# A graph network on one core: the TensorE share of the row fetch is dealt over another chunk's work, with more columns, and reaches the edge network

## The chip, the cores and the metric

One core of a Trainium2 chip runs the kernel. The metric is the device time of one execution in microseconds (us). A core has TensorE (PE, with its weight loads shown apart as PEld), VectorE (DVE), ScalarE (ACT), GpSimd (POOL) and SyncE (SP); each works through its own instructions in order, and semaphores join them. The profile shows one execution.

## The reference

The graph has 12,500 nodes with 32 features and 400,000 edges, sorted by their destination. Three attention layers run one after the other, then a LayerNorm with the residual, then an edge network with a maximum over each node's edges, then a second LayerNorm.

```python
def _gat(x, edge_index, W, att_s, att_d, bias, heads, ch, neg_slope):
    h = (x @ W.T).reshape(n, heads, ch)
    a_s = (h * att_s[None]).sum(-1)
    a_d = (h * att_d[None]).sum(-1)
    logits = leaky_relu(a_s[src] + a_d[dst], neg_slope)
    m = segment_max(logits, dst)
    ex = exp(logits - m[dst])
    denom = segment_sum(ex, dst)
    alpha = ex / (denom[dst] + 1e-16)
    out = segment_sum(alpha[:, :, None] * h[src], dst)
    return out.reshape(n, heads * ch) + bias
...
h = _gat(x, ..., heads=2, ch=16)      # then scale, elu, clip
h = _gat(h, ..., heads=2, ch=16)      # then elu, clip
x = layernorm(x + _gat(h, ..., heads=1, ch=32))
e_feat = concatenate([x[src], x[dst], edge_attr])
v = relu(e_feat @ W1 + b1) @ W2 + b2
x = layernorm(x + maximum(segment_max(v, dst), x))
```

## The kernel before

**Tiling.** Edge `p*3125 + t` lies in partition `p`, column `t`. A *column* is thus 128 edges, one in each partition, and there are 3125 of them. Every stage works through the columns in 54 *chunks*: 50 of 60 columns, then 48, 32, 29 and 16. Since the edges are sorted by destination, segment sums and maxima are scans along a partition, carried from chunk to chunk; layer 2 and the edge network walk backwards, so that the runs of one layer end where those of the next begin.

**The fetch.** For each column a layer needs the row of each edge's source: h and the scores, 36, 34 or 33 numbers in layers 1 to 3, and 32 numbers in the edge network (buffer `xs`). There are two ways to get it.

- `gather` (L71): one indirect DMA on POOL per column, 128 rows from a table in memory.
- `Fetch` (L221 to L275), for one column in `EVERY`: all 98 x 128 node rows are held in SBUF as `by_group`, three bf16 parts in 7 groups. A matmul with the identity lays the sources out as a row (L255, fp32, two passes); DVE compares them into one-hot weights `oh` (L258); 21 bf16 matmuls, 7 groups by 3 parts, add up into the PSUM tile `acc` (L270); DVE masks out the right one of 14 rows, `mine` (L273), and reduces it into the column's place in the buffer (L275). With its weight loads a column is 46 PE instructions.

`by_group` is filled from x ahead of layer 1 and by `node_groups` (98 gathers and the splitting into parts) ahead of layers 2 and 3.

**A layer** is `attention`. The function `rows_of(c + 1)` issues the gathers of the next chunk into one of three buffers `g`, and then calls `fetch`, which writes all PE columns of that chunk in one block, ahead of the present chunk's own operations. Then chunk c is worked on: scores, running maximum, exponentials, the weighted rows `gf` (L833, one for each head, the last reader of `g`), their scans (L839), the sums' rows copied out (L842 and what follows it), and `finish`: division, bias, ELU, and for blocks of 16 columns the product with the next layer's weights (`ph`, L620) and attention vectors (`pa`, L621). Layer 3 ends in `finish3` and `layernorm` in place of the products. A buffer `g` may be filled again when its L833 is through.

**The edge network**, `edge_network`, fetches every column on POOL, into one of four buffers `xs`. For each chunk DVE spreads the destination's rows over its edges with scans (`xf`, L958 and L968), then, for each block of 16 columns, turns three inputs (`xt` L974, `et` L975, `xst` L976), PE multiplies them (`ph`, L981, twelve passes and as many weight loads with the two halves of the hidden layer), ACT applies the relu (`ht`, L983), PE makes `pv` (L987), DVE turns it back (L988). After the blocks come the maximum scans (L991), the result (L906 to L908) and the LayerNorm (L633 to L641).

**Order.** The engines' orders come from a scheduler that works on the program's order, so that part of a block of columns is found between the present chunk's operations. Within an engine the order is then fixed, and an instruction that waits holds up those behind it.

Of the kernel before, what the change touches and what calls it, by code (L numbers as in the profile page):

```python
# [24 lines left out]
def gnn_resnorm_kernel(ctx: ExitStack, tc: tile.TileContext, a: dict, out: bass.AP):  # L25
# [24 lines left out]
    T = 60  # L50
# [39 lines left out]
    EVERY = {1: 7, 2: 7, 3: 7}  # L90
# [18 lines left out]
    runs = ctx.enter_context(tc.tile_pool(name="runs", bufs=1))  # L109
    gstack = ctx.enter_context(ExitStack())  # L110
    xpool = gstack.enter_context(tc.tile_pool(name="x", bufs=1, side="right"))
    by_group = xpool.tile([P, 3, KT, KN * (D + 4)], BF16, name="by_group")
# [36 lines left out]
    zeros = const.tile([P, 500], F32, name="zeros")  # L149
# [70 lines left out]

    class Fetch:  # L221
# [22 lines left out]
        def fetch(self, psum, g, t0, n, bufs=2):  # L244

            todo = [t for t in range(t0, t0 + n) if t in self]
            if not todo:
                return
            pool, w, i0 = self.pool, self.w, todo[0] // self.every
            bm = pool.tile([P, 9, KN], F32, name="bm")[:, :len(todo), :]  # L250
            nc.vector.tensor_tensor(bm, bcast(count[:, None, :KN], [P, len(todo), KN]),
                                    bcast(self.b[:, i0:i0 + len(todo), None], [P, len(todo), KN]), op=ALU.is_equal)

            def ones_of(m):
                nc.tensor.matmul(places_p, lhsT=bcast(self.at[:, i0 + m:i0 + m + 1], [P, P]), rhs=ident,  # L255
                                 start=True, stop=True)
                oh = pool.tile([P, KT, P], BF16, name="oh")
                nc.vector.tensor_tensor(oh, bcast(places_p[:, None, :], [P, KT, P]),  # L258
                                        bcast(kid[:, :, None], [P, KT, P]), op=ALU.is_equal)
                return oh  # L260

            coming = ones_of(0)
            for m, t in enumerate(todo):
                oh = coming
                if m + 1 < len(todo):
                    coming = ones_of(m + 1)
                acc = psum.tile([P, 512], F32, name="acc", bufs=bufs)[:, :KN * w]
                for k in range(KT):
                    for i in range(3):
                        nc.tensor.matmul(acc, lhsT=oh[:, k, :], rhs=by_group[:, i, k, :KN * w],  # L270
                                         start=(k == i == 0), stop=(k == KT - 1 and i == 2))
                mine = pool.tile([P, D + 4, KN], F32, name="mine")[:, :w, :]
                nc.vector.tensor_mul(mine, acc.rearrange("p (w b) -> p w b", b=KN),  # L273
                                     bcast(bm[:, m:m + 1, :], [P, w, KN]))
                nc.vector.tensor_reduce(g[:, t - t0, :w], mine, axis=AX.X, op=ALU.add)  # L275
# [22 lines left out]
    def clear(table, part=0, parts=1):  # L298
        flat = edge_rows(table).rearrange("p t w -> p (t w)")
        k = TE * table.shape[1] // parts  # L300
        z = next(z for z in range(500, 0, -1) if k % z == 0)
        tc.keep_in_program_order(
            nc.sync.dma_start(out=flat[:, part * k:part * k + k].rearrange("p (k z) -> p k z", z=z),
                              in_=bcast(zeros[:, None, :z], [P, k // z, z])))
# [290 lines left out]
    def finish(li, pool, psum, den, v, n):  # L595
# [8 lines left out]
        nc.scalar.activation(e, e, AF.Exp, scale=-1.0)  # L604
        heads = HEADS[li + 1]
# [3 lines left out]
        for b in range(0, n, TB):  # L609
            nt = min(TB, n - b)  # L610
            w = nt * D
            pe = psum.tile([P, TB * D], F32, name="pe")[:, :w].rearrange("p (f t) -> p f t", t=nt)
            nc.scalar.activation(pe, e[:, :, b:b + nt], AF.Identity, bias=minus[:, 1:2])
            yb = pool.tile([P, TB * D], F32, name="yb", bufs=1)[:, :w].rearrange("p (f t) -> p f t", t=nt)
            nc.vector.scalar_tensor_tensor(yb, y[:, :, b:b + nt], 3.0, pe, op0=ALU.min, op1=ALU.add)
            yt = pool.tile([P, TB * D], F32, name="yt")[:, :w]
            nc.vector.transpose(blocks(yt), yb.rearrange("p f t -> p t f"))  # L617
            ph = psum.tile([P, TB * D], F32, name="ph")[:, :w]
            pa = psum.tile([P, TB * D], F32, name="pa")[:, :w]
            nc.tensor.matmul(ph, lhsT=w_bd, rhs=yt, start=True, stop=True)  # L620
            nc.tensor.matmul(pa, lhsT=a_bd, rhs=yt, start=True, stop=True)  # L621
            at = pool.tile([P, TB, D], F32, name="at", bufs=1)[:, :nt, :]
            nc.vector.transpose(tb[:, b:b + nt, :D], blocks(ph))  # L623
            nc.vector.transpose(at, blocks(pa))  # L624
            nc.scalar.copy(tb[:, b:b + nt, D:], at[:, :, :heads])  # L625
            nc.scalar.copy(ta[:, b:b + nt, :], at[:, :, heads:2 * heads])
        return tb, ta

    def layernorm(lp, st, x, n, sq=None):
# [4 lines left out]
        nc.vector.tensor_scalar(st, st, 1.0 / D, None, op0=ALU.mult)  # L634
        nc.vector.tensor_sub(x, x, bcast(st[:, :, None], [P, n, D]))
        nc.scalar.activation(sq, x, AF.Square)
        nc.vector.tensor_reduce(st, sq, axis=AX.X, op=ALU.add)
        nc.vector.tensor_scalar(st, st, 1.0 / D, EPS, op0=ALU.mult, op1=ALU.add)
        nc.scalar.activation(st, st, AF.Sqrt)
        nc.vector.reciprocal(st, st)  # L640
        nc.vector.tensor_mul(x, x, bcast(st[:, :, None], [P, n, D]))  # L641

    def finish3(pool, psum, den, v, x, n):

        y = psum.tile([P, D * 64], F32, name="y3")[:, :D * n].rearrange("p (f t) -> p f t", t=n)
        divided(3, y, den, v, n)
        nc.vector.tensor_add(x, x, y.rearrange("p f t -> p t f"))
        layernorm(pool, den[:, T:], x, n)
# [73 lines left out]
    def attention(li, idx):  # L722
# [10 lines left out]
        with ExitStack() as stack:  # L733
# [23 lines left out]
            with tc.tile_pool(name=f"ps{li}", bufs=1, space=PSUM) as psp, \  # L757
                    tc.tile_pool(name=f"fps{li}", bufs=1, space=PSUM) as fps:
                den = small_p[:, 128:]
                def rows_of(c):  # L760
# [5 lines left out]
                    fetch.fetch(psp, g, t0, n)  # L766
                    return g
# [3 lines left out]
                for c, (t0, n) in enumerate(todo):  # L771
                    g = coming
                    if c + 1 < len(todo):
                        coming = rows_of(c + 1)
                    (ad, xr) = loaded
# [28 lines left out]
                    nc.vector.scalar_tensor_tensor(lg, lg, slope, lg, op0=ALU.mult, op1=ALU.max)  # L804
                    if c == 0:
# [14 lines left out]
                    nc.scalar.activation(wt, lg, AF.Exp)  # L820

# [6 lines left out]
                    for h in range(heads):  # L828
# [6 lines left out]
                        nc.scalar.copy(v[:, h * wd + ch, cur], wt[:, h, :])  # L835
                        for f in range(0, wd, FS):
# [3 lines left out]
                                                         turned(gf[:, o:o + k], rev), 0.0, op0=ALU.mult, op1=ALU.add)  # L840
                    rows = sp.tile([P, T, gw + heads], F32, name="rows", bufs=1)[:, :n, :]
# [5 lines left out]
                    if li < 3:  # L847
                        tb, ta = finish(li, fp, fps, den, v[:, :, cur], n)
                        nc.sync.dma_start(out=edge_rows(gives[li + 1])[:, t0:t0 + n, :], in_=ta)
                    else:  # L850
                        finish3(fp, fps, den, v[:, :, cur], xr, n)
# [58 lines left out]
    def edge_network(tag, in_order):  # L910


        with tc.tile_pool(name=f"in{tag}", bufs=2) as ip, tc.tile_pool(name=f"gx{tag}", bufs=4) as gp, \
                tc.tile_pool(name=f"v{tag}", bufs=2) as vp, tc.tile_pool(name=f"t{tag}", bufs=2) as tp, \
                tc.tile_pool(name=f"pf{tag}", bufs=1, space=PSUM) as pfp, \
                tc.tile_pool(name=f"ph{tag}", bufs=1, space=PSUM) as php:
# [15 lines left out]

            old = None
            loaded = load(0)
            for c, (t0, n) in enumerate(todo):
                xs = gp.tile([P, T, D], F32, name="xs")
                for t in range(n):
                    gather(xs[:, t, :], tables[4], src_last[:, t0 + t:t0 + t + 1])
# [9 lines left out]
                rf = pfp.tile([P, FS * (T + 1)], F32, name="rf")[:, :FS * m]  # L948
                cft = cf.rearrange("p (k t) -> p k t", t=m)
                rft = rf.rearrange("p (k t) -> p k t", t=m)  # L950
# [4 lines left out]
                nc.vector.memset(rft[:, :, n:], -BIG)  # L955
                nc.scalar.copy(cft[:, :, :n], ct)
                nc.vector.tensor_scalar(rft[:, :, :n], ct, -1.0, BIG, op0=ALU.add, op1=ALU.mult)
                nc.vector.tensor_mul(xft[:, :, :n].rearrange("p f t -> p t f"), xd, bcast(keep[:, :, None], [P, n, D]))  # L958
                if old is None:
# [6 lines left out]
                for f in range(0, D, FS):  # L966
                    fs = slice(f * m, (f + FS) * m)
                    nc.vector.tensor_tensor_scan(turned(xf[:, fs], True), turned(cf, True), turned(xf[:, fs], True), 0.0,  # L968
                                                 op0=ALU.mult, op1=ALU.add)
                for b in range(0, n, TB):  # L970
# [7 lines left out]
                    for h in range(2):  # L978
# [5 lines left out]
                        hts.append(ht)  # L984
                    pv = php.tile([P, TB * D], F32, name="pv")[:, :w]
                    for h in range(2):
                        nc.tensor.matmul(pv, lhsT=w2_bd[:, h, :], rhs=hts[h], start=(h == 0), stop=(h == 1))  # L987
                    nc.vector.transpose(vft[:, :, b:b + nt].rearrange("p f t -> p t f"), blocks(pv))  # L988
                for f in range(0, D, FS):
                    fs = slice(f * m, (f + FS) * m)  # L990
                    nc.vector.tensor_tensor_scan(turned(vf[:, fs], True), turned(rf, True), turned(vf[:, fs], True), 0.0,  # L991
                                                 op0=ALU.add, op1=ALU.max)
                nc.scalar.copy(xd, vft[:, :, :n].rearrange("p f t -> p t f"))
# [9 lines left out]
                layernorm(tp, small_p[:, 128:], z, n)  # L1003
# [58 lines left out]
```

## Time and profile before

| what | us |
|---|---|
| median of 10 executions | 22450.19 |
| lowest and highest | 22433.18 and 22474.39 |
| the profiled execution | 22439.96 |
| its span | 22438.2 |
| setup, up to the first chunk of layer 1 | 0 to 316 |
| layer 1 | 316 to 6150 |
| layer 2 | 6300 to 12126 |
| layer 3 | 12255 to 17535 |
| edge network | 17535 to 22300 |
| merge of the partition ends, rows out to the nodes | 22300 to 22438 |

The stretches between the layers are the filling of `by_group`. In the lists of the profile, a group of instructions shows the line, the engine, the operation, out<-in by the program's names, partitions x elements, and the count; then busy us, the mean ns of one, and after the second bar the idle time of the engine just before these instructions with what ended most of it. In a timeline a row has start and length in us, and in brackets the idle time before it and what ended it. "remote" and "issue" mean that nothing which the profile shows released the instruction. The ends of matmuls are modelled. The granted clock is TensorE's, as a share of full speed.

Two rows on the fetch, beside those that come below:

```profile
L270 PE MATMUL acc<-by_group,oh 128*128 128x504 bf16 (+2 forms) x28098 | 6637.7, 393 | 683.0 <-issue 673.2
L258 DVE TENSOR_TENSOR oh<-fixed,kid 128x896 bf16<-128x896 f32 x1338 | 1446.1, 1081 | 222.8 <-remote 96.9
```

### The profile page before, as it was taken

The numbers are of one execution on the slowest core, as the hardware profiler recorded it, in microseconds if no ns is written. First come the engines' busy times: TensorE is split into PE (matmuls) and PEld (weight loads), VectorE is DVE, ScalarE is ACT, GpSimd is POOL, SyncE is SP. The second block draws the span as 40 slices with busy tenths as digits, with TensorE's granted clock in tenths as the row PEclk, the third lists the DMA queues.
The fourth block names the chain that finished last, engine by engine and source line by source line (L and its number), as shares of the span: only waits on it lengthen the run. The fifth ranks groups of instructions, "written<-read, shape, count | busy, mean of one in ns | idle before, by whom it ended". The sixth has DMA issues, their size and how long they took to land.

```text
span 22438.2 us, 107898 instructions
## 1 busy us (share of the span) xinstructions
PE 9727.2 (43%) x35914; PEld 4508.6 (20%) x35914; DVE 9821.6 (44%) x13987; ACT 2921.2 (13%) x3898; POOL 11186.0 (50%) x11780
## 2 busy tenths in 40 slices
PE   1545555454534444444443344444444233333332
PEld 0222222222212222222221122222222111111111
DVE  2444444444524444444443344444444345555554
ACT  0111111111101111111111010101101111111111
POOL 6444444444354444444445544545444666666663
PEclk5777777777767777777776676676767666666666
DMA  3111111111101111111111111111111111111111
GB/s 50 45 38 38 49 38 38 39 40 29 34 17 28 28 28 30 28 28 30 28 28 31 31 40 37 42 36 42 38 39 41 45 48 59 55 59 55 59 55 43
DMA packets 562459, 881.63 MB, mean 39 GB/s; under 512 B 267999, under 2 KB 482494, under 8 KB 548446
## 3 DMA queue, kind: packets, MB, share of 16 engines
q1 hardware_dynamic: 185036, 665.01, 8.2%
q0 software_dynamic: 376544, 206.39, 6.3%
q8 instruction: 285, 4.67, 0.1%
q10 hardware_dynamic: 304, 3.20, 0.0%
q14 instruction: 290, 2.37, 0.0%
HBM read 370.51 MB, written 503.27 MB: 39 GB/s over the span
## 4 chain that ended last, share of the span: by engine, by line
another core or an unknown queue 34%; DVE 24%; PE 24%; issue 10%; ACT 4%; POOL 3%; DMA 1%; DVEq 0%; SPq 0%; POOLq 0%; ACTq 0%
PE acc L270 15%; PE ph L981 3%; DVE gf L833 3%; DVE gf L839 3%; PE pv L987 1%; DVE oh L258 1%; DVE yt L617 1%; PE ph L620 1%; DVE y L589 1%; DVE mine L273 1%; PE pa L621 1%; PE fixed L255 1%; DVE y L593 1%; DVE z L908 1%
## 5 line engine op out<-in xcount | busy, mean ns | idle before, releaser
L270 PE MATMUL acc<-by_group,oh 128*128 128x504 bf16 (+2 forms) x28098 | 6637.7, 393 | 683.0 <-issue 673.2
L71 POOL DMA_INDIRECT g<-table,src_i x2679 | 2532.5, 945 | 3195.9 <-DVE gf L833 2369.4
L71 POOL DMA_INDIRECT g<-table,src_last x2679 | 2541.8, 949 | 3153.0 <-DVE gf L833 2351.5
L71 POOL DMA_INDIRECT g<-table,src_first x2679 | 2538.3, 947 | 2660.7 <-DVE gf L833 1858.9
L71 POOL DMA_INDIRECT xs<-table,src_last x3125 | 2978.9, 953 | 1585.0 <-issue 941.1
L270 PEld LDWEIGHTS <-oh 128*128 128x128 bf16 x28098 | 2941.6, 105 | 4085.0 <-issue 1747.7
L273 DVE TENSOR_TENSOR mine<-acc,bm 128x504 f32<-128x504 f32 (+2 forms) x1338 | 873.7, 653 | 5614.6 <-remote 3503.2
L255 PE MATMUL fixed<-ident,fat 128*128 128x128 f32 x2676 | 665.1, 336 | 4030.9 <-DVE oh L258 1421.1
L620 PE MATMUL ph<-yt,w_bd 128*128 128x512 f32 (+2 forms) x840 | 613.0, 822 | 4137.1 <-issue 2709.6
L258 DVE TENSOR_TENSOR oh<-fixed,kid 128x896 bf16<-128x896 f32 x1338 | 1446.1, 1081 | 222.8 <-remote 96.9
L981 PE MATMUL ph<-xt,wb_bd 128*128 128x512 f32 (+2 forms) x832 | 505.0, 694 | 2327.5 <-issue 1253.5
L623 DVE STREAM_TRANSPOSE tb<-ph 128x512 f32<-128x512 f32 (+2 forms) x420 | 284.4, 677 | 2674.0 <-remote 2117.5
L255 PEld LDWEIGHTS fixed<-ident,fat 128*128 128x128 f32 x2676 | 553.8, 224 | 4367.5 <-issue 2701.5
L620 PEld LDWEIGHTS ph<-yt,w_bd 128*128 128x128 f32 x840 | 179.9, 250 | 4279.0 <-issue 3862.8
L275 DVE TENSOR_REDUCE g<-mine 128x36 f32<-128x504 f32 (+2 forms) x1338 | 848.4, 634 | 0.1
L987 PE MATMUL pv<-ht,w_bd 128*128 128x512 f32 (+2 forms) x832 | 520.9, 727 | 705.6 <-ACT ht L983 546.3
L820 ACT ACTIVATE fixed<-lg 128x120 f32<-128x120 f32 (+3 forms) x162 | 41.2, 254 | 5645.9 <-DVE oh L258 5645.5
L839 DVE TENSOR_TENSOR_SCAN gf<-rx,gf 128x488 f32<-128x488 f32 (+4 forms) x918 | 756.6, 867 | 5.5
L621 PE MATMUL pa<-yt,a_bd 128*128 128x512 f32 (+2 forms) x840 | 596.1, 802 | 323.6 <-DVE at L624 274.2
L981 PEld LDWEIGHTS ph<-xt,wb_bd 128*128 128x128 f32 x832 | 188.2, 234 | 2576.6 <-issue 1497.4
L842 ACT COPY rows<-gf 128x2040 f32<-128x2040 f32 (+3 forms) x162 | 628.5, 3880 | 558.6 <-DVE gf L839 555.8
L625 ACT COPY tb<-at 128x32 f32<-128x32 f32 (+4 forms) x420 | 92.3, 220 | 4415.0 <-DVE at L624 4019.1
(333 smaller groups left out, 10843.6 us busy)
## 6 DMA issues: line engine op xcount, KB each, us to landing
sums<-rows SPq DMA_DIRECT2D x100, 1080.0 KB
table<-tb SPq DMA_DIRECT2D x50, 1020.0 KB
sums<-rows SPq DMA_DIRECT2D x50, 1020.0 KB
x_e<-zeros SPq DMA_DIRECT2D x10, 5000.0 KB
xs<-table,src_last POOLq DMA_INDIRECT x3125
table<-tb SPq DMA_DIRECT2D x50, 990.0 KB
xr<-x_e SPq DMA_DIRECT2D x50, 960.0 KB
table<-xr SPq DMA_DIRECT2D x50, 960.0 KB
```

The lines of the kernel that those rows point to most:

```text
L71: return nc.gpsimd.indirect_dma_start(out=dst, out_offset=None, in_=table, in_offset=bass.IndirectOffsetOnAxis(ap=idx, axis=0))
L255: nc.tensor.matmul(places_p, lhsT=bcast(self.at[:, i0 + m:i0 + m + 1], [P, P]), rhs=ident, start=True, stop=True)
L258: nc.vector.tensor_tensor(oh, bcast(places_p[:, None, :], [P, KT, P]), bcast(kid[:, :, None], [P, KT, P]), op=ALU.is_equal)
L270: nc.tensor.matmul(acc, lhsT=oh[:, k, :], rhs=by_group[:, i, k, :KN * w], start=(k == i == 0), stop=(k == KT - 1 and i == 2))
L273: nc.vector.tensor_mul(mine, acc.rearrange("p (w b) -> p w b", b=KN), bcast(bm[:, m:m + 1, :], [P, w, KN]))
L275: nc.vector.tensor_reduce(g[:, t - t0, :w], mine, axis=AX.X, op=ALU.add)
L620: nc.tensor.matmul(ph, lhsT=w_bd, rhs=yt, start=True, stop=True)
L621: nc.tensor.matmul(pa, lhsT=a_bd, rhs=yt, start=True, stop=True)
L833: nc.vector.tensor_mul(v[:, h * wd:h * wd + ch, cur].rearrange("p f t -> p t f"), g[:, :, h * ch:(h + 1) * ch], bcast(wt[:, h, :, None], [ ...
L839: nc.vector.tensor_tensor_scan(turned(gf[:, o:o + k], rev), turned(rx[:, :k], rev), turned(gf[:, o:o + k], rev), 0.0, op0=ALU.mult, op1=AL ...
L981: nc.tensor.matmul(ph, lhsT=wb_bd[:, s, h, :], rhs=x, start=(s == 1), stop=(s == 0))
L987: nc.tensor.matmul(pv, lhsT=w2_bd[:, h, :], rhs=hts[h], start=(h == 0), stop=(h == 1))
```

## The change

- One column in 6 goes to PE in layers 1 and 2 and one in 5 in layer 3, in place of one in 7; the edge network, which had none, gets one in 12.
- `fetch` becomes `columns`. It returns a `Paced` object, whose steps are: the one-hot of the next column, the matmuls of this one, and the select (mask and reduction) of the one before. The present chunk's code calls `step()` at points between its operations, and the steps are spread evenly over these points. The first chunk's columns are all done at once (`rest()`).
- The edge network gets `rows_of`, one chunk ahead, with three buffers `xs` in place of four, and `node_groups` ahead of its first chunk. `by_group` moves into a pool that lives to the end.
- In the edge network a block's `pv` is turned back one block late; `rf` shares a PSUM tile with `cf` and is made after the blocks; the LayerNorm's squares go into `ea`.
- The tile of zeros has 250 columns in place of 500, `bm` has room for 12 columns.

```diff
-    EVERY = {1: 7, 2: 7, 3: 7}
+    EVERY = {1: 6, 2: 6, 3: 5, 4: 12}
...
+    class Paced:
+        def __init__(self, steps, count):
+            self.steps, self.count, self.taken, self.passed = steps, count, 0, 0
+        def at_points(self, points):
+            self.points = points
+            return self
+        def __call__(self):
+            self.passed += 1
+            while self.taken < min(self.count, -(-self.count * self.passed // self.points)):
+                next(self.steps)
+                self.taken += 1
+        def rest(self):
+            for _ in self.steps:
+                pass
...
-            coming = ones_of(0)
-            for m, t in enumerate(todo):
-                oh = coming
-                if m + 1 < len(todo):
-                    coming = ones_of(m + 1)
-                acc = psum.tile([P, 512], F32, name="acc", bufs=bufs)[:, :KN * w]
...
-                nc.vector.tensor_reduce(g[:, t - t0, :w], mine, axis=AX.X, op=ALU.add)
+            def select(m, acc, bm):
+                mine = pool.tile([P, D + 4, KN], F32, name="mine")[:, :w, :]
+                nc.vector.tensor_mul(mine, acc.rearrange("p (w b) -> p w b", b=KN),
+                                     bcast(bm[:, m:m + 1, :], [P, w, KN]))
+                nc.vector.tensor_reduce(g[:, todo[m] - t0, :w], mine, axis=AX.X, op=ALU.add)
+            def steps():
...
+                oh, acc = ones_of(0), None
+                for m in range(len(todo)):
+                    coming = ones_of(m + 1) if m + 1 < len(todo) else None
+                    done, acc = acc, psum.tile([P, 512], F32, name="acc", bufs=2)[:, :KN * w]
+                    for k in range(KT):
+                        for i in range(3):
+                            nc.tensor.matmul(acc, lhsT=oh[:, k, :], rhs=by_group[:, i, k, :KN * w],
+                                             start=(k == i == 0), stop=(k == KT - 1 and i == 2))
+                    if m:
+                        select(m - 1, done, bm)
+                    oh = coming
+                    yield
+                select(len(todo) - 1, acc, bm)
+                yield
+            return Paced(steps(), len(todo) + 1)
...
                 for c, (t0, n) in enumerate(todo):
-                    g = coming
+                    g, step = coming
+                    step.rest()
+                    step = alone
                     if c + 1 < len(todo):
                         coming = rows_of(c + 1)
+                        step = coming[1].at_points(2 + 2 * heads + (1 + -(-n // TB) if li < 3 else 5))
```

Where the points lie in a layer: after the scores, after the exponentials, for each head after its weighted rows and after its scans; then in `finish` after the ELU's parts and after each block's two products, or in `finish3` after the division, after the sum and three times in `layernorm`. In the edge network:

```diff
+            fetch = Fetch(stack, f"k{tag}", EVERY[4], D)
+            node_groups(4, last_i, D)
...
+                    step = coming[1].at_points(9 + 2 * -(-n // TB))
...
                 nc.vector.tensor_mul(xft[:, :, :n].rearrange("p f t -> p t f"), xd, bcast(keep[:, :, None], [P, n, D]))
+                step()
...
+                step()
+                late = []
                 for b in range(0, n, TB):
...
+                    step()
+                    if late:
+                        nc.vector.transpose(*late)
                     pv = php.tile([P, TB * D], F32, name="pv")[:, :w]
...
-                    nc.vector.transpose(vft[:, :, b:b + nt].rearrange("p f t -> p t f"), blocks(pv))
+                    step()
+                    late = (vft[:, :, b:b + nt].rearrange("p f t -> p t f"), blocks(pv))
+                rf = pfp.tile([P, FS * (T + 1)], F32, name="cf")[:, :FS * m]
...
+                nc.vector.transpose(*late)
+                step()
...
-                layernorm(tp, small_p[:, 128:], z, n)
+                layernorm(tp, small_p[:, 128:], z, n, ea, step)
```

The other points there lie after the maximum scans, twice in the result's loop, and three times in `layernorm`.

## The prediction

> **What bounds the kernel now.** I read the page first: shares by engine, the chain that ended last, and the costliest groups.
>
> ```profile
> PE 9727.2 (43%) x35914; PEld 4508.6 (20%) x35914; DVE 9821.6 (44%) x13987; ACT 2921.2 (13%) x3898; POOL 11186.0 (50%) x11780
> ...
> another core or an unknown queue 34%; DVE 24%; PE 24%; issue 10%; ACT 4%; POOL 3%; DMA 1%; DVEq 0%; SPq 0%; POOLq 0%; ACTq 0%
> ...
> L71 POOL DMA_INDIRECT g<-table,src_i x2679 | 2532.5, 945 | 3195.9 <-DVE gf L833 2369.4
> ...
> L71 POOL DMA_INDIRECT xs<-table,src_last x3125 | 2978.9, 953 | 1585.0 <-issue 941.1
> ...
> L273 DVE TENSOR_TENSOR mine<-acc,bm 128x504 f32<-128x504 f32 (+2 forms) x1338 | 873.7, 653 | 5614.6 <-remote 3503.2
> ```
>
> No engine is full, and a third of the chain is put down to something unseen. POOL idles until L833 has read a buffer g; DVE stands 5.6 ms before L273, which needs a finished column, over half of it released by nothing visible. Next PE's timeline, once while the gathers run and once when POOL is idle (start, length, operation, last field the idle time before):
>
> ```profile
> 6390.58 0.55 PE L270 MATMUL acc<-by_group,oh 128*128 128x476 bf16 x1 [2.25 <-issue]
> 6393.38 0.55 PE L270 MATMUL acc<-by_group,oh 128*128 128x476 bf16 x1 [2.25 <-issue]
> 6396.18 0.55 PE L270 MATMUL acc<-by_group,oh 128*128 128x476 bf16 x1 [2.25 <-issue]
> ...
> 6557.66 4.38 PE L270 MATMUL acc<-by_group,oh 128*128 128x476 bf16 x21
> ```
>
> While gathers run, a weight load with its matmul takes 2.80 us (6393.38 to 6396.18): 1.40 us per PE instruction. With POOL idle the whole column of 21 pairs takes 4.38 us. DVE's timeline of the same stretch gives the column:
>
> ```profile
> 6358.39 0.65 DVE L273 TENSOR_TENSOR mine<-acc,bm 128x476 f32<-128x476 f32 x1 [43.05 <-remote]
> 6422.79 0.66 DVE L273 TENSOR_TENSOR mine<-acc,bm 128x476 f32<-128x476 f32 x1 [56.44 <-remote]
> ...
> 6562.08 0.65 DVE L273 TENSOR_TENSOR mine<-acc,bm 128x476 f32<-128x476 f32 x1 [2.23 <-PE acc L270]
> 6566.52 0.65 DVE L273 TENSOR_TENSOR mine<-acc,bm 128x476 f32<-128x476 f32 x1 [2.23 <-PE acc L270]
> ```
>
> 64.40 us against 4.44 us. A column is 46 PE instructions (2+2 at L255, 21+21 at L270), and 46 x 1.40 = 64.4. It isn't the matmul's size: in the first edge chunk a block of 32 fp32 instructions ends at 17839 after 17794.5, 44.5/32 = 1.39. Then the clog by stages, in windows of one chunk each (a gather burst, then the pause after it; length, busy times of PE, weight loads, DVE, ACT, POOL, granted clock, DMA share, GB/s):
>
> ```profile
> 3043.60:3108.20 64.60, 17.86 (x47) 7.16 (x47) 20.24 (x41) 13.68 (x13) 49.05 (x52) 0.63 0.15 33
> 3108.20:3156.70 48.50, 40.65 (x176) 19.28 (x176) 28.01 (x36) 1.68 (x9) 0.01 (x1) 0.86 0.06 24
> 14031.00:14096.00 65.00, 15.46 (x61) 7.06 (x58) 26.41 (x37) 9.36 (x8) 49.14 (x52) 0.63 0.22 60
> 14096.00:14134.00 38.00, 30.57 (x147) 15.98 (x148) 18.91 (x23) 0.22 (x1) 0.00 (x0) 0.82 0.00 1
> 18918.80:18993.40 74.60, 28.79 (x60) 12.29 (x59) 42.73 (x46) 12.71 (x15) 56.57 (x60) 0.68 0.22 66
> 18993.40:19005.10 11.70, 3.22 (x7) 1.34 (x6) 2.96 (x4) 1.26 (x2) 0.02 (x1) 0.81 0.01 1
> ```
>
> In layers 1 and 3 PE does a quarter or so of its matmuls in the long burst and the rest in the short pause: the pause is where the kernel lives, a burst is mostly standing. Only the first 15 us of a burst are unhindered (an edge block's pv is 0.04 us late up to there, 2.3 to 4.8 us at 17 to 20 us, 7 to 8 us at its end), and the hold outlasts the last gather by 5 to 9 us; I take 6. The edge network is the exception: no columns, so it lives almost inside its burst, 74.6 + 11.7 = 86.3 us a chunk. Mean chunk periods, from the starts of POOL's bursts: 110 us in layers 1 and 2, 100.2 in layer 3, 86.3 in the edge network. 3125/60 = 52.1 full chunks per stage.
>
> **The change, part by part.** POOL has 945 ns and a 0.30 us gap for each gather, 1.246 us.
>
> *Layers 1 and 2.* 520 columns by PE instead of 446: a chunk of 60 has 10 columns and 50 gathers, burst 62.3 us, hold over at 68.3. Columns no longer precede the chunk's work but are dealt over it; the release (L833) now stands behind about half of them. From the release, the free 15 us hold the next columns: three to four at 4.4 to 4.7 us. The one after needs 46 x 1.40 us and takes the rest of the burst; DVE runs in order, its next select waits on that column, and behind it wait the scores, L833 and so the next release. After the hold: 5 columns x 4.69 (POOL idle, 504 wide) = 23.5; four ph and pa pairs, 8.2; two L833 with their scans, 6.3; a first column at the low clock 8.8 instead of 4.69, +4.1. The scores hide under the columns. 68.3 + 42.1 = 110.4 against 110: nothing. Its bounds are 6 us a chunk either way (one column more or less after the hold), x 104 = 625 us.
>
> *Layer 3.* 625 columns instead of 446: 12 columns, 48 gathers, burst 59.8, hold over at 65.8. Four columns fit the free window, one stands in the hold, seven are left at 4.32: 30.2. Cold start 4.1, the scaled copy of rows out (L879 after, 3.8), scans 4.4. Sum 108.3 against 100.2: +8.1 x 52.1 = +420 us. Bounds: 0 (scans and copy hidden) and +600.
>
> *Edge network, grouping.* 98 gathers and the grouping ahead of its first chunk: the same for layer 3 took 12126.8 to 12252.5, 125.7 us. Nothing hides it: the first columns read the groups. +126.
>
> *Edge network, columns.* 5 of 60 columns go to PE, 55 gathers, burst 68.4, hold over at 74.4. The buffer is released by the last xst transpose of a chunk. At that point PE owes, in the new order: pv of block 2, a column, block 3, pv, block 4, a column, pv, a column: about 200 instructions. 15 us let some 80 through (pv 2.1, column 4.4, block 5.2, pv 2.1 = 13.8); 60 us at 1.40 another 42; DVE waits in order at the transposes and selects. The rest falls after the hold. Then DVE's tail, from L991 at 19023.4 to the end of L641 at 19054.1: 30.7; xf and its scans, 3.8 + 4.4; two oh at 1.08; a cold column 7.8; block 1 5.2; column 4.4; pv 2.1; block 2 5.2, and the next release. 74.4 + 30.7 + 8.2 + 2.2 + 7.8 + 5.2 + 4.4 + 2.1 + 5.2 = 140.2. Against 86.3: +53.9 x 52.1 = +2810 us. The DVE tail ran inside the burst before, at no cost; now it runs after it. From below: if the hold let everything through, POOL's 68.4 would bound it, -930 us; the nearest row that has columns beside gathers is layer 3's, 100.2, giving +720. From above 146, +3110. I take 140, since the layers' rows show columns in gathers at 64 us.
>
> *Small edits at nothing*: one oh fewer hidden, rf after the blocks, one transpose late, the LayerNorm's shared scratch, smaller zeros: under 1 us of DVE a chunk, each beside a hold of 50 us; uncovered, 52 us in all. Extra selects (0.65 + 0.63) and oh (1.08) are inside the column times.
>
> Sum: 126 + 0 + 420 + 2810 = +3356. The profiled execution took 22439.96 us (span 22438.2), 10 us under the median 22450.19, inside the runs' 22433 to 22474. 22450 + 3356 = 25,806; I say 25,800.
>
> Weighed against a rule: PE's 1.40 us per instruction stands while DMA moves 33 to 66 GB/s. The Trainium skill, "SBUF — State Buffer", section "SBUF: two separate sides", has engine and DMA ports disjoint; by it columns would take 4.4 us beside gathers, and the change would go the way of the faster rival. The measured 64.4 us contradicts that reading. Also, L270 takes 0.42 us at a granted clock of 0.5 and 0.21 warm; "TensorE: Matmul & The Clock Gate", section "Why this matters for your kernels", says idle gaps let the clock fall, which speaks against dealing columns between other work.
>
> **Rivals.** *A, the edge network's hold is milder.* If its three owed columns slip into the free window or 30 more instructions pass, DVE's tail runs in the burst as before. For it: in 18918.8 to 18993.4 PE did 60 of 67 matmuls inside the burst. Against: those fit because 119 instructions, some 70 of them in the free window, were all there was. Chunk at 92 to 104 us: +300 to +920, with 126 and 0 to 420, 22,900 to 23,900.
>
> *B, faster.* Dealing lets DVE work in the burst. Each select comes one point after its column, so while PE crawls through a column DVE may do scores, scans and copies; today it does 20.2 us of its 48.3 us there (layer 1). If 40 us of them fit, a chunk of layers 1 and 2 falls by 20 us to 90 (-2080), layer 3's by 10 (-520), and the edge network, at 100, adds 714 and 126: 20,700. It decides from 840/156 = 5.4 us saved a layer chunk, if the edge network stays at 100; with 140 it needs 19. For it: columns ahead of the chunk's operations are what DVE stands behind now. Against: two columns in a row cannot end inside one burst, and the selects come at every point, some 5 us of DVE apart.
>
> *C, no change*: 587 gathers fewer x 1.246 = 731 us, balance a mild edge loss. Only a mixture gives it.
>
> **How the numbers follow.** Main case 0.68, own range 24,900 to 26,700 (terms' bounds, not all at one end). A 0.14, C 0.03, B 0.15, spread from 17,900 to 22,400. The range 22,700 to 26,900 takes in A and the main case, and leaves B and C out. A measurement of this kernel can't tell 0.2%, 45 us, from no change: faster 0.15, same 0.03, slower 0.82.
>
> **What would show it.** Right: edge bursts of 55 gathers followed by some 70 us of idle POOL, DVE's L641 after the burst's last gather, columns of 4.3 to 4.7 us in pauses and above 40 us in bursts, "remote" before the select in the edge network too; layer periods near 110, 110 and 108. Wrong: edge periods under 105, or DVE busy over 25 us in a layer 1 burst. My hold is measured on blocks of columns in a row; were it milder for single columns between other work, every step above shrinks.

## The result, and the profile after

The changed kernel took 26,472 us (median of 8, 26,448 to 26,498) against 22,453 us of the kernel before beside it: a ratio of 1.179, interval 1.178 to 1.180. Forecast were 25,800 us, range 22,700 to 26,900.

From the page of the changed kernel (shares by engine, the chain, two groups):

```profile
PE 12303.5 (47%) x49415; PEld 5756.9 (22%) x49415; DVE 11167.6 (42%) x15836; ACT 2961.9 (11%) x3919; POOL 10689.4 (40%) x11291
...
another core or an unknown queue 10%; PE 7%; DVE 7%; issue 2%; POOL 2%; ACT 1%; DMA 0%; DVEq 0%; ACTq 0%; POOLq 0%
...
L287 DVE TENSOR_TENSOR mine<-acc,bm 128x462 f32<-128x462 f32 (+3 forms) x1925 | 1243.1, 646 | 9155.7 <-remote 7165.5
L71 POOL DMA_INDIRECT xs<-table,src_last x2865 | 2711.3, 946 | 4543.6 <-DVE xst L1040 3606.5
```

POOL works less (10,689 us, was 11,186) and its share falls from 50% to 40%. The wait of the select (L287, formerly L273) on something unseen has doubled, 3,503 to 7,166 us, and POOL, which stood 0.6 ms for the edge network's buffers before (until L976), now stands 3.6 ms until the last transpose L1040 frees one. (The chain's shares sum to 29% here; it could not be followed through the rest.)

Windows of the changed kernel, burst and pause of one chunk in layer 1, layer 3 and the edge network (columns as before):

```profile
3093.80:3155.90 62.10, 15.39 (x71) 7.17 (x69) 13.52 (x18) 10.28 (x6) 47.16 (x50) 0.65 0.15 33
3155.90:3207.10 51.20, 42.02 (x177) 19.83 (x177) 36.56 (x62) 5.26 (x17) 0.01 (x1) 0.90 0.06 24
13979.10:14038.70 59.60, 22.18 (x90) 9.66 (x90) 13.80 (x18) 3.99 (x2) 45.26 (x48) 0.65 0.15 31
14038.70:14095.20 56.50, 40.01 (x186) 20.38 (x186) 39.33 (x51) 5.89 (x8) 0.04 (x2) 0.83 0.10 36
20005.80:20074.20 68.40, 30.68 (x98) 13.14 (x98) 8.41 (x10) 2.53 (x4) 51.87 (x55) 0.69 0.08 13
20074.20:20146.90 72.70, 26.23 (x83) 11.89 (x82) 48.47 (x56) 11.45 (x13) 0.00 (x0) 0.63 0.15 54
```

The edge network is the change: DVE did 42.7 us of its work inside a burst and does 8.4 now; the pause grew from 11.7 to 72.7 us. In layers 1 and 3, too, DVE does less in the burst than before (13.5 for 20.2, 13.8 for 26.4).

By stage, from the first gather of each to that of the next, in us:

| stage | before | after | change | forecast |
|---|---|---|---|---|
| layers 1 and 2 | 11,938.6 | 12,361.0 | +422 | 0 (625 either way) |
| layer 3 | 5,284.0 | 6,097.6 | +814 | +420 |
| edge network with its grouping | 4,764.0 | 7,534.7 | +2,771 | +2,936 |
| setup and end | | | +3 | 0 |

### The profile page after: what moved, and what is told of

The parts are those of the page before. It is cut to its first block, busy times and chain, and to the rows that moved or that the text cites. A ratio compares the mean times of both kernels' runs of the same rounds, so it can differ in the third digit from the quotient of the medians.

```text
span 26447.6 us, 136746 instructions
## 1 busy us (share of the span) xinstructions
PE 12303.5 (47%) x49415; PEld 5756.9 (22%) x49415; DVE 11167.6 (42%) x15836; ACT 2961.9 (11%) x3919; POOL 10689.4 (40%) x11291
## 5 line engine op out<-in xcount | busy, mean ns | idle before, releaser
L301 PE MATMUL acc<-by_group,oh 128*128 128x462 bf16 (+3 forms) x40425 | 9615.6, 392 | 2864.6 <-issue 2656.0
L301 PEld LDWEIGHTS <-oh 128*128 128x128 bf16 x40425 | 4189.4, 104 | 7706.7 <-issue 4224.4
L278 PE MATMUL fixed<-ident,fat 128*128 128x128 f32 x3850 | 1004.3, 349 | 9985.5 <-DVE oh L281 6502.0
L287 DVE TENSOR_TENSOR mine<-acc,bm 128x462 f32<-128x462 f32 (+3 forms) x1925 | 1243.1, 646 | 9155.7 <-remote 7165.5
L71 POOL DMA_INDIRECT xs<-table,src_last x2865 | 2711.3, 946 | 4543.6 <-DVE xst L1040 3606.5
L281 DVE TENSOR_TENSOR oh<-fixed,kid 128x896 bf16<-128x896 f32 x1925 | 2081.1, 1081 | 3099.1 <-remote 2712.8
L289 DVE TENSOR_REDUCE g<-mine 128x33 f32<-128x462 f32 (+2 forms) x1665 | 1061.2, 637 | 3.6
L649 ACT ACTIVATE pe<-e,minus 128x512 f32<-128x512 f32 (+2 forms) x420 | 278.1, 662 | 5269.9 <-DVE yb L651 5246.7
L879 DVE TENSOR_TENSOR gf<-g,fixed 128x960 f32<-128x960 f32 (+5 forms) x270 | 604.2, 2238 | 1.6 <-ACT fixed L865 1.2
L1047 ACT ACTIVATE ht<-ph,b_c 128x512 f32<-128x512 f32 (+2 forms) x416 | 274.8, 661 | 2809.9 <-PE ph L1045 1521.8
```

The source lines that it names most:

```text
L71: return nc.gpsimd.indirect_dma_start(out=dst, out_offset=None, in_=table, in_offset=bass.IndirectOffsetOnAxis(ap=idx, axis=0))
L289: nc.vector.tensor_reduce(g[:, todo[m] - t0, :w], mine, axis=AX.X, op=ALU.add)
L879: nc.vector.tensor_mul(v[:, h * wd:h * wd + ch, cur].rearrange("p f t -> p t f"), g[:, :, h * ch:(h + 1) * ch], bcast(wt[:, h, :, None], [ ...
```

## The experiments

The kernel before was timed on every chip that was used. It took 22,453 us beside the result above, 22,172 us on the chip of the first four runs, 22,164 on that of the last two (no columns once more, and one point more with the hold), but 15,006 and 15,025 us on two other chips, on which the gathers do not hold PE (shown in the last section). "The hold" is the stretch in which PE takes 1.40 us an instruction beside the gathers. Results are compared within one kind of chip. Even within one kind layers 1 and 2 differ: the run with plain rows, whose layers are those of the changed kernel, has periods of 109.4 and 111.7 us there, the changed kernel 113.5 and 115.1 beside its result. So their periods are compared on one chip only; layer 3's and the edge network's agree to 0.4 us.

**Edge network without columns** (chip with the hold)

```diff
-    EVERY = {1: 6, 2: 6, 3: 5, 4: 12}
+    EVERY = {1: 6, 2: 6, 3: 5, 4: 0}
-            node_groups(4, last_i, D)
```

> The changed kernel, with no column of the edge network on PE and without the grouping ahead of it; the new order of the edge network and its three buffers stay. Theory (gathers hold PE, and the columns' 230 instructions a chunk push DVE's tail out of the burst): the edge network's period goes from 141.7 us back to about 87 (84 to 95), its bursts to 60 gathers with some 12 us of idle POOL, and the whole to 26,450 - 54 x 52.1 - 126 = about 23,500 us. Rival (the reordering of the edge network, late transposes and three buffers, costs it): the period stays above 110 us and the whole above 24,700.

Measured: 23,228 us (one run); bursts of 60 gathers, 11.3 us of idle POOL, period 85.9, the same as the next two runs show with the edge network of the kernel before (86.0 and 85.9). The edge network's loss comes with its columns and their grouping; late transposes and three buffers cost nothing that shows.

**The block order with the higher counts** (same chip)

```diff
-    EVERY = {1: 7, 2: 7, 3: 7}
+    EVERY = {1: 6, 2: 6, 3: 5}
-            bm = pool.tile([P, 9, KN], F32, name="bm")[:, :len(todo), :]
+            bm = pool.tile([P, 12, KN], F32, name="bm")[:, :len(todo), :]
-    zeros = const.tile([P, 500], F32, name="zeros")
+    zeros = const.tile([P, 250], F32, name="zeros")
...
-        z = next(z for z in range(500, 0, -1) if k % z == 0)
+        z = next(z for z in range(250, 0, -1) if k % z == 0)
```

> The kernel before, with its block order of columns, but one column in six, six and five on PE, and zeros of 250. Theory (the count of columns is what lengthens the layers; dealing is worth little): layers 1 and 2 gain 1.43 columns x 4.69 less 1.8 us of burst, 110 to 115 us; layer 3 gains 3.43 x 4.32 less 4.4, 100.4 to 111; edge network unchanged at 86; the whole 22,450 + 4.9 x 104 + 10.5 x 52 = 23,500 us. Rival (the dealing is what costs): periods stay within 3 us of 110 and 100, the whole under 22,800.

Measured: 23,181 us (one run), 1,009 us over the kernel before on this chip, where the theory had 1,050; periods 111.5, 112.2, 110.5. The run above has the same counts and deals: 109.2, 112.1, 116.0. So the counts make the loss of the whole, and in layer 3 its period too (110.5 for an expected 111); dealing gains 2 us in layer 1, nothing in layer 2, and costs 5.5 us in layer 3. Layers 1 and 2 came out 3 us under the expectation, inside the 3 us that the rival had given; as their 110 us come from another chip, their periods don't decide between the two.

**No columns on PE** (same chip, then once more on another)

```diff
-    EVERY = {1: 7, 2: 7, 3: 7}
+    EVERY = {1: 0, 2: 0, 3: 0}
```

> The kernel before, with no column on PE at all: POOL gathers all 60 of a chunk. Theory (the columns stand in the gathers' hold and fill the pauses, POOL alone would be the bound): bursts of 60 x 1.246 = 74.8 us, almost no idle POOL, periods of 75 to 85 us in layers 1 to 3, 86 in the edge network, both fillings between the layers (2 x 126 us) gone: 22,450 - 30 x 104 - 20 x 52 - 252 = 18,000 us, range 17,200 to 19,200. Rival (the columns relieve POOL, and other waits, not PE's hold, make the pause): each period grows by the nine gathers added, 11 us, to about 121 and 111: 24,000 us.

Measured: 18,524 us, 0.835 of the kernel before (0.834 to 0.837). From its page:

```profile
PE 2952.4 (16%) x5140; PEld 1150.3 (6%) x5140; DVE 6900.4 (37%) x9723; ACT 2909.2 (16%) x3856; POOL 13325.0 (72%) x12922
...
POOL 55%; issue 22%; DVE 8%; another core or an unknown queue 6%; PE 6%; ACT 2%; DMA 1%; DVEq 0%; POOLq 0%; ACTq 0%
```

POOL heads the chain, and the layers run at its pace: 3125 gathers between 314.7 and 4685.2 us, 83.9 us for 60. On these chips the kernel is 16% shorter without the PE fetch: it saves nine gathers a chunk, and puts some 390 PE instructions where most of them must wait for POOL to stop. This version beats both kernels there.

> The kernel before with no column on PE, once more. On a chip with the hold (kernel before near 22,200 to 22,450): 0.83 to 0.84 of it. On a chip without the hold (kernel before near 15,000, one layer chunk of 51.4 gathers about 64 us): nine more gathers a chunk in three layers, each 1.25 to 1.40 us, 11 to 20 us a chunk, less the two fillings (252 us): 16,500 to 17,900, slower than the kernel before.

A chip with the hold again: 18,525 us, 0.836 (0.834 to 0.837). It has not been run on the other kind of chip. An estimate for that kind, where the run with one column in seven shows gathers at 1.25 us: 1,338 more gathers are 1,670 us, the fillings left out 252, so some 1,400 us more than the kernel before.

**Plain rows for the edge network's gathers** (chip with the hold; the rows fetched are not the sources')

```diff
-                for t in range(n):
-                    if t0 + t not in fetch:
-                        gather(xs[:, t, :], tables[4], src_last[:, t0 + t:t0 + t + 1])
+                nc.sync.dma_start(out=xs[:, :n, :], in_=edge_rows(tables[4])[:, t0:t0 + n, :])
```

> The changed kernel, but the edge network's POOL gathers are replaced by one plain DMA of a chunk's rows (other rows than the sources': that part of the computation is changed); its columns on PE, their order and their DVE work stay. Theory (the gathers hold PE): without gathers no column takes over 10 us, the period falls from 141.7 us to DVE's and PE's own, 70 to 85 us, and the whole to about 23,300 us. Rival (columns dealt between the blocks cost by their own waits and the cold clock): the period stays above 120 us.

Measured: 23,158 us (one run). From DVE's timeline, one operation a chunk and two selects between:

```profile
20014.50 2.15 DVE L681 TENSOR_TENSOR z<-z,fixed 128x1920 f32<-128x1920 f32 x1
...
20031.47 0.62 DVE L287 TENSOR_TENSOR mine<-acc,bm 128x448 f32<-128x448 f32 x1 [1.54 <-PE acc L301]
20040.81 0.62 DVE L287 TENSOR_TENSOR mine<-acc,bm 128x448 f32<-128x448 f32 x1 [2.51 <-PE acc L301]
...
20099.83 2.15 DVE L681 TENSOR_TENSOR z<-z,fixed 128x1920 f32<-128x1920 f32 x1
```

A period of 85.33 us (20014.50 to 20099.83), with all five columns and their DVE work. That is 0.3 us over the range of the theory and far from the rival's 120. So the same chunk costs 141.6 us beside gathers and 85.3 without: 56.3 us go with the gathers. The waits before the selects are 1.5 and 2.5 us, where a chunk of the changed kernel has one of 38.8 (shown further down), and are released by a PE that can be seen.

**Rows from scattered places, without POOL** (chip without the hold; other rows again)

```diff
-                nc.sync.dma_start(out=xs[:, :n, :], in_=edge_rows(tables[4])[:, t0:t0 + n, :])
+                nc.sync.dma_start(out=xs[:, :n, :], in_=tables[4][0:E, :].rearrange("(t p) w -> p t w", p=P)[:, t0:t0 + n, :])
```

> As the run with plain rows (other rows than the sources' in the edge network, and no gathers there), but the DMA takes each row of 128 bytes from another place, so that it moves as many small packets a chunk as the gathers did, without POOL. If the small packets hold PE: selects tens of us apart while the DMA runs, period over 100 us. If only POOL's gathers do: period 85 us as with plain rows, columns under 10 us.

Measured: 15,328 us, period 85.3. Where gathers hold nothing, this decides nothing: whether small packets or POOL's own issuing holds PE stays open. The changed kernel's trace shows that the hold outlasts both: over 43 edge chunks the last DMA packet of the gathers' queue ends 1.1 us (median) after POOL's last gather, but the first select comes 9.1 us after it (8.4 to 9.2). So PE is still behind some 8 us after the last packet that the trace shows.

**Fourteen matmuls a column** (twice on chips without the hold; the third part is left out of the sum)

```diff
-                        for i in range(3):
+                        for i in range(2):
...
-                                             start=(k == i == 0), stop=(k == KT - 1 and i == 2))
+                                             start=(k == i == 0), stop=(k == KT - 1 and i == 1))
```

> The changed kernel with two of the three bf16 parts in a column's matmuls: 14 in place of 21, so 32 PE instructions a column in place of 46 (the third part of each row is left out of the sum). Theory (in the gathers' hold PE takes 1.40 us an instruction): in the long gathers at the start of a layer the selects lie 32 x 1.40 = 44.8 us apart, not 64.4; in the edge network 70 fewer instructions a chunk leave less behind the hold, period 141.7 to about 130 (125 to 136). Rival (a column in the hold takes a burst's time because something else, such as the select or the wait for a buffer, is tied to the gathers): the selects stay 64 us apart.

> The kernel with 14 matmuls a column (32 PE instructions; the third part of each row is left out of the sum) once more. On a chip with the hold, theory (1.40 us a PE instruction): selects in the long gathers at a layer's start 32 x 1.40 = 44.8 us apart; edge period 125 to 136. Rival (a burst's time whatever the column holds): 64 us apart. On a chip without the hold it tells nothing of this and repeats 14,870 us.

Measured: 14,870 and 14,887 us, edge period 78.6. The question was about the hold, so it wasn't answered. That the hold goes by instructions rests on two places of the trace before and not on an experiment: 46 in 64.4 us, and 32 in 44.9. The edge period tells something else: 35 matmuls fewer a chunk, with their weight loads, take 6.7 us off the 85.3 of the run below, so on this kind of chip the columns' matmuls stand in the row that sets the period.

**One column in seven, dealt** (chip without the hold)

```diff
-    EVERY = {1: 6, 2: 6, 3: 5, 4: 12}
+    EVERY = {1: 7, 2: 7, 3: 7, 4: 0}
-            node_groups(4, last_i, D)
```

> The changed kernel with one column in seven in the three layers, as before, and none in the edge network: the dealing alone. Theory (dealing moves the columns but the burst still lets through about four, and one stands in it): layers 1 and 2 within 3 us of the kernel before (110), layer 3 3 to 7 us over its 100.4, since the columns' row is broken where one chunk's steps end and the next begin; edge 86; the whole between the kernel before and 400 us over it. Rival 1 (dealing is a gain that the higher counts hide): layers 1 to 3 each 5 us or more under it. Rival 2 (dealing costs everywhere): each 5 us or more over it.

Measured: 14,962 us against 15,006, one run each: no more than 0.3%. The theories spoke of the hold, so neither they nor the rivals were tested; on this chip POOL has 69% of the chain, and the order of the columns hides behind it.

**The changed kernel on a chip without the hold**

> The changed kernel once more. The last four runs showed a chip where gathers do not hold PE: the kernel before took 15,006 us there, POOL was its bound, and selects lay under 10 us apart beside running gathers. On a chip with the hold (kernel before near 22,200 to 22,450): 1.17 to 1.19 of the kernel before, edge period 140 to 142. On a chip without it: layers bound by 50 and 48 gathers a chunk, 62 to 65 us; the edge network by PE and DVE in a row, 79 to 84 us, against 75 before; grouping +126; the whole 14,900 to 15,200, within 1.5% of the kernel before.

Measured: 15,360 us against 15,025, ratio 1.022 (1.019 to 1.025), above the upper bound I gave. DVE's timeline:

```profile
11538.71 2.15 DVE L681 TENSOR_TENSOR z<-z,fixed 128x1920 f32<-128x1920 f32 x1
...
11624.05 2.15 DVE L681 TENSOR_TENSOR z<-z,fixed 128x1920 f32<-128x1920 f32 x1
```

85.34 us a chunk, the 85.33 of the run with plain rows on the other kind of chip: the edge chunk's own row of DVE and PE steps, with gathers that hold nothing or with none. Without columns (next experiment) the period is 74.9 us, 60 gathers of 1.25: the columns take 5 gathers from POOL, and put DVE and PE in its place, 10 us longer. So the edge network's columns with their grouping lose on both kinds: its stage takes 4,633 us here against 3,993 in the next experiment, 640 us more, and 2,771 more there.

**One point more at the start of a layer's chunk**

```diff
-    EVERY = {1: 6, 2: 6, 3: 5, 4: 12}
+    EVERY = {1: 6, 2: 6, 3: 5, 4: 0}
-            node_groups(4, last_i, D)
...
-                        step = coming[1].at_points(2 + 2 * heads + (1 + -(-n // TB) if li < 3 else 5))
+                        step = coming[1].at_points(3 + 2 * heads + (1 + -(-n // TB) if li < 3 else 5))
...
                         clear(x_e, c // 4, 10)
+                    step()
```

> The changed kernel without columns in the edge network, and with one more point, at the very start of a layer's chunk ahead of its scores. Theory (layer 3 came out 7.7 us over my sum because the row of columns runs dry where a chunk's steps end: 13.2 us between two selects in place of 4.3): layer 3's period falls from 116.0 to 108 to 113, layers 1 and 2 by 0 to 4 us from 109.2 and 112.1, the whole from 23,228 by 150 to 600 us. Rival (layer 3's excess lies in DVE's LayerNorm after the hold): no change over 1 us in any period.

> The changed kernel without columns in the edge network and with one more point at the start of a layer's chunk. On a chip with the hold, theory (layer 3's row of columns runs dry at the chunk's end): layer 3's period 108 to 113 us in place of 116.0; rival (the LayerNorm after the hold): within 1 us of 116. On a chip without the hold: 14,740 us again, 0.975 to 0.99 of the kernel before, with the edge network back at 75 us.

Measured without the hold: 14,738 us against 15,006 (one run each), edge period 75: higher counts and dealing in the layers alone, with the extra point, look like a gain of 1.8% there. With the hold: 23,063 us, 1.040 (1.038 to 1.042); periods 108.3, 109.7 and 115.9 against 109.2, 112.1 and 116.0 of the run without columns in the edge network. Layer 3 didn't move, so the point does not mend it, and my expectation for it fell; the rival's "within 1 us of 116" came true. Layers 1 and 2 (0.9 and 2.4 us less) and the whole (165 less) fell as expected, but between two chips. The gap is still there (selects at 15079.08 and 15092.56): on DVE the new point lies behind the LayerNorm's last product, as the old first one did.

## Why the prediction was right

**The hold.** At a layer's start, where the gathers of several chunks run on, the changed kernel's selects lie as far apart as before; DVE's timeline:

```profile
6592.66 0.65 DVE L287 TENSOR_TENSOR mine<-acc,bm 128x476 f32<-128x476 f32 x1 [56.48 <-remote]
6657.06 0.65 DVE L287 TENSOR_TENSOR mine<-acc,bm 128x476 f32<-128x476 f32 x1 [57.15 <-remote]
```

64.40 us. The prediction's second place, 32 instructions in 44.5 us, is 44.9 by PE's rows (two `pv` of the first edge chunk before, L987, start at 17790.40 and 17835.28); that is 1.40 us each, as for the column. Rival B needed single columns between other work to be spared; they weren't, and DVE's time in a layer 1 burst fell to 13.5 us where the rival wanted 40, and the prediction's sign of being wrong over 25.

**Edge network.** Forecast 140.2 us a chunk, measured 141.6 (140.9 to 142.6); 55 gathers in 68.4 us, 73 us of idle POOL. The parts of the sum can be read off one chunk whose burst starts at 20005.8:

```profile
20037.74 0.71 DVE L1040 STREAM_TRANSPOSE xst<-xs 128x512 f32<-128x512 f32 x1 [4.24 <-remote]
20043.40 1.09 DVE L281 TENSOR_TENSOR oh<-fixed,kid 128x896 bf16<-128x896 f32 x1 [4.94 <-remote]
20083.32 0.63 DVE L287 TENSOR_TENSOR mine<-acc,bm 128x448 f32<-128x448 f32 x1 [38.83 <-remote]
...
20114.08 2.15 DVE L681 TENSOR_TENSOR z<-z,fixed 128x1920 f32<-128x1920 f32 x1
...
20146.10 0.58 DVE L1040 STREAM_TRANSPOSE xst<-xs 128x384 f32<-128x384 f32 x1 [0.28 <-PE ph L1045]
```

DVE's last wait of the hold ends 77.5 us after the burst's start (74.4 in the sum); the LayerNorm ends at 20116.2, 32.9 us on (30.7 in the sum); the transpose that frees the buffer ends at 20146.7, 30.5 us on (35.1 in the sum). So the mechanism is as forecast, but that the total came within 1.4 us is partly luck: parts that missed by +3.1, +2.2 and -4.6 us nearly cancel. The stage grew by 165 us less than the sum. Its steady part agrees; the difference lies at the two ends, which the sum took as steady. The second and third chunk took 195 us each before, in the stage's long first burst, and 141 after, and the last three full chunks, as the gathers run out, took 126, 105 and 104 us after. Rival A, a period of 92 to 104, did not come.

**Layer 3** was mis-sized: forecast 108.3 us a chunk, measured 116.0 on average and 116.1 in the one told here; the stage's +814 us lie outside the bounds that were given (0 to +600). The hold ended at 64.8 us, a microsecond early. After it came 51.3 us, not 42.5: eight columns were left, not seven (+4.3); the scans lie behind the release and not before it (-4.4); and between two selects (14071.55 and 14084.73) lie 13.2 us in place of 4.3 (+8.9). PE's timeline has that place:

```profile
14063.14 8.35 PE L301 MATMUL acc<-by_group,oh 128*128 128x462 bf16 x42
14076.04 0.80 PE L278 MATMUL fixed<-ident,fat 128*128 128x128 f32 x2 [4.55 <-DVE xr L681]
14078.05 0.80 PE L278 MATMUL fixed<-ident,fat 128*128 128x128 f32 x2 [1.21 <-DVE oh L281]
```

One chunk's steps are used up while the LayerNorm still runs; the next chunk's first identity matmul waits for the LayerNorm's last product, then come one-hot and 21 matmuls in a row. This reading of the trace adds up; the one experiment on it changed nothing, so what would remove the gap is not shown.

**Layers 1 and 2** were forecast at no change and lost 3 and 5 us a chunk, +422, inside the 625 given. In the chunk of layer 1 shown above the hold ended at 67.6 us (forecast 68.3), and then seven selects came before the release, not five; only three columns had fitted the burst's first 15 us.

The whole came out 672 us over the forecast's 25,800, by the layers (+422, and +814 for +420), less what the edge network fell short of its sum. The edge network carries two thirds of the loss; the forecast had it at nearly nine tenths.

**What did not depend on the hold** was left out of my cases: the edge chunk's own 85.3 us of DVE and PE steps, above the 75 us of 60 gathers. With it the change is a loss of 2.2% even where gathers hold nothing. The prediction's lower bound, the 68.4 us of POOL if the hold let everything through, could therefore not be reached.

## What to carry to other kernels

Before giving an idle engine a share of a bound engine's work, look at how long its instructions take while the bound engine runs, not at its busy share: here a column cost 4.4 us beside an idle POOL and 64.4 us beside a busy one. Try the version that leaves the sharing out altogether, and on the chip where it is to run; it was 16% shorter than the kernel before on the chips with the hold, and would by the estimate above be longer on the others. And sum up one chunk's own chain: once it is longer than the bound engine's time, taking more from that engine is a loss in any case.

## What the runs showed of the hardware

The same program, the kernel before, took 22,164 to 22,453 us on some chips and 15,006 to 15,025 us on two others. The changed kernel took 26,472 and 15,360. What differs is the hold. On a chip without it, PE's and POOL's timelines of the changed kernel:

```profile
4004.61 4.38 PE L301 MATMUL acc<-by_group,oh 128*128 128x476 bf16 x21
...
4009.05 4.38 PE L301 MATMUL acc<-by_group,oh 128*128 128x476 bf16 x21
```

```profile
4005.15 0.94 POOL L71 DMA_INDIRECT g<-table,src_last  x1 [0.30 <-issue]
4006.40 0.95 POOL L71 DMA_INDIRECT g<-table,src_last  x1 [0.30 <-issue]
4007.65 0.94 POOL L71 DMA_INDIRECT g<-table,src_last  x1 [0.30 <-issue]
```

Gathers at the same 1.25 us, and 4.4 us a column beside them. Its list of waits has no "remote" before the selects:

```profile
DVE mine L287 <- PE acc L301: 1509.5, 781, 5.4
```

The Trainium skill, "SBUF — State Buffer", section "SBUF: two separate sides", says that engine ports and DMA ports are disjoint, so that a DMA and a compute operation cannot slow each other. These rows agree, 4.44 us a column beside gathers. On the other chips a column took 64.40 us beside them; no run shows whether that happens at the ports. What makes a chip one or the other no run here tells.

The packed traces part the two kinds in one more way. In the changed kernel's trace without the hold an indirect DMA leaves 16 records of its landing (179,845 for 11,278); in its trace with the hold there are 2.5 (28,149 for 11,278). All six traces without the hold have 15.9 to 16.0, all eight with it 1.8 to 3.1. So where the hold is, records are missing too. That is a rival which no run here tests: whether the hold belongs to the gathers or to the recording of them.

Second, gathers that follow each other without a pause slow down where the hold is: 1.40 us each on average over layer 1 of the version without columns (3125 in 4370.5 us), 1.25 in bursts of 50 to 60. The 1.40 is a mean and its agreement with the time of one PE instruction in the hold may be chance: 61% of these gathers come less than 1.33 us after the one before, 26% at about 1.40, the rest later, and the first 180 in a row of layers 2 and 3 and of the edge network take 1.26 each. On a chip without the hold (one column in seven, dealt) 2,679 in a row took 1.25 us each. Whether the two are one thing is open.
